# A scan layer of five engines: source order kept on every engine, preparation cut in pieces, one activation table set, pipelined epilogue

**Chip, cores, metric.** One core of a Trainium2 chip. The metric is the device time of one execution in microseconds (us), the lower the better. Executions of one kernel agree within 0.3%. The engines are named as in the profile: PE (TensorE, matrix products), DVE (VectorE), ACT (ScalarE), POOL (GpSimd) and SP (SyncE, which here issues DMA transfers). PSUM is the memory in which this kernel keeps PE's products.

## The reference, cut to what matters

Layer 0 is a two-dimensional selective scan (4 images of 48 x 48 tokens, 256 channels, 16 states, 4 scan directions). Layer 1 (attention, then spectral filters) is not touched by the change.

```python
xz = einsum('bhwc,ec->bhwe', groupnorm(x), in_proj_w); xin, z = split(xz, 2)
xc = silu(conv3x3_depthwise(xin) + conv_b)
xs = [xc in four scan orders]                       # rows, columns, and both reversed
dts_r, Bs, Cs = split(x_proj_w @ xs)
dt = softplus(dt_proj_w @ dts_r + dt_proj_b)
step: h = h * exp(dt*A) + (dt*u) * B ;  y = sum_n h * C      # along 2304 tokens
y  = sum of the four orders + D*xs
x  = x + out_proj(layernorm(y) * g + b) * silu(z))           # the epilogue
```

## The kernel before

The layer is cut into 80 *chunks* (image, direction, 480 or 384 tokens). A chunk is 8 *units* (half `h` of the channels, group `q` of 4 states). In a unit the engines work in turn: ACT makes `dA = exp(dt*A)`, DVE or POOL makes `s = dt*u*B`, DVE scans, POOL multiplies by C, PE sums over states, DVE adds to `ya`. Step sizes of the next chunk but one are prepared meanwhile, and go through DRAM to be replicated over partitions.

```python
psy = ... bufs=1 (PSUM) ; psm = ... bufs=3 (PSUM) ; s has 6 buffers

def prep(self):                      # a generator, advanced one yield per unit
    ps = x_proj @ xc;  yield
    xd = Identity(ps);  dma(bcd <- xd[32:64])                       # B and C rows to DRAM
    for h in range(NH):
        ps = dt_proj @ xd;  yield
        re[:,h,1] = Abs(ps); re[:,h,0] = Relu(ps)
    e = Exp(-e); u = e + 1;  yield
    l = Ln(u);  u = u - 1
    for h in range(NH):
        ps = e - u + l + relu   (4 matmuls);  yield                 # softplus, on PE
        re[:,h,0] = copy(ps)                                        # ACT
        re[:,h,1] = ps * x                                          # DVE
        dma(d[h] <- re[:,h]);  for c in range(4): dma(rep[h] <- d[h], replicated)   # 2 MB

def fetch(self, i):                  # broadcast row i of bcd to 128 partitions: 4 DMA issues
    t = one.tile([P, CS], tag=f"bc{i}"); ...

def enter(self):                     # unit s+2 on POOL for 3 of 8 units, else s+1 on DVE
    s = sp.tile(...)
    nc.scalar.copy(ch.entry(s), carry)                              # L344
    eng.tensor_tensor(s, rep[h][:, 1], B, mult)                     # L347
def scan(self):
    for j in range(2):
        2 x activation(dA[j], rep[h][:, 0], Exp, scale=A)           # L355
        tensor_tensor_scan(s, dA[j], s)                             # L359
def leave(self):
    nc.scalar.copy(carry, s end)                                    # L366
    nc.gpsimd.tensor_tensor(s, s, C row, mult)                      # L369
    4 x matmul(y, csum, s)                                          # L373
```

Lines are cut and shortened. All DMAs of the layer but the loads of its weights at the start are issued by SyncE (SP), one queue.

The softmax here doesn't subtract the row's maximum and nothing guards it: scores larger than these inputs give would overflow.

## Time and profile before

| | before |
|---|---|
| time, median of 3 runs | 9344.46 us |
| scan layer, start to the attention's first tokens | 5642 us |
| chunk of 480 tokens, mean of steady ones | 65.6 us |
| DVE busy in 66.03 us of such a chunk | 47.19 us |
| change of image, above three steady chunks | 111 us |

The chunk times come from the starts of the first scans of neighbouring chunks in the trace. A chunk is *steady* when it is not one of the last two of an image or the first of the next; those three together are the change of image. The lines themselves are in the prediction.

### The profile page before, as it was taken

Reading aid. Unit: us, or ns where it says so; the run is one execution under the profiler, and the core shown is the slowest. Engines: PE = TensorE matmul, PEld = TensorE weight load, DVE = VectorE, ACT = ScalarE, POOL = GpSimd, SP = SyncE. Lnnn points to the kernel's source line nnn. Section 1 sums busy time; section 2 is a strip of 40 time slices with the busy share of each in tenths; the row PEclk is TensorE's granted clock in tenths of the full one; section 3 lists DMA queues with packets and bytes.
Section 4 is the critical chain, followed back from the end, with each engine's and each line's share of the span. In section 5 each row is a group of like instructions: output and inputs, shape, how many; then the busy total and the mean of one; then the engine's idle time right before and its main releaser. Section 6 shows DMA issues by size and latency. Waiting matters only on the chain. (4 is left out here: it accounts for less than half of the span.)

```text
span 9358.5 us, 64225 instructions
## 1 busy us (share of the span) xinstructions
PE 6679.6 (71%) x22344; PEld 3265.5 (35%) x22344; DVE 4675.9 (50%) x3928; ACT 3151.3 (34%) x6187; POOL 3540.9 (38%) x984
## 2 busy tenths in 40 slices
PE   4555545555546555546555548979999999999999
PEld 1111112111112111112111114547666666666666
DVE  6777677677677776777776772021111111111111
ACT  4444445444445444445444433430000000000000
POOL 3666655666655666655666660010000000000000
PEclk6656556656556555557555559989999999999999
DMA  4434434434434434434434430000000000000000
GB/s 103 98 87 103 93 76 104 102 88 103 96 73 106 103 85 103 97 72 109 103 84 104 101 80 31 0 11 7 9 8 8 15 8 8 8 15 6 6 6 21
DMA packets 378087, 571.07 MB, mean 61 GB/s; under 512 B 50841, under 2 KB 373529, under 8 KB 377762
## 3 DMA queue, kind: packets, MB, share of 16 engines
q1 hardware_dynamic: 374784, 566.19, 26.4%
q8 instruction: 176, 2.88, 0.1%
q14 instruction: 149, 1.22, 0.0%
q10 hardware_dynamic: 2978, 0.77, 0.0%
HBM read 467.68 MB, written 99.09 MB: 61 GB/s over the span
## 5 line engine op out<-in xcount | busy, mean ns | idle before, releaser
L369 POOL TENSOR_TENSOR s<-s,bc 128x1920 f32<-128x1920 f32 (+1 forms) x640 | 2431.4, 3801 | 1904.3 <-ACT carry L366 1386.1
L359 DVE TENSOR_TENSOR_SCAN s<-dA,s 128x962 f32<-128x962 f32 (+1 forms) x1536 | 2606.7, 1744 | 434.5 <-ACT dA L355 283.7
L731 PE MATMUL cv<-tt,u 128*128 128x384 f32 (+2 forms) x9216 | 2505.5, 433 | 0.0
L373 PE MATMUL y<-s,csum 128*32 128x480 f32 (+1 forms) x5120 | 1066.9, 923 | 1344.9 <-POOL s L369 1251.2
L355 ACT ACTIVATE dA<-rep,A 128x480 f32<-128x480 f32 (+1 forms) x2560 | 1618.3, 643 | 1030.6 <-DVE s L359 999.0
L731 PEld LDWEIGHTS cv<-tt,u 128*128 128x128 f32 x9216 | 1648.7, 190 | 869.7
L737 DVE COPY U<-cv 128x384 f32<-128x384 f32 x384 | 214.0, 557 | 2245.1 <-PE cv L731 2245.1
L735 ACT COPY U<-cv 128x384 f32<-128x384 f32 x384 | 183.6, 478 | 2797.3 <-PE cv L731 2797.3
L712 POOL TENSOR_TENSOR ms<-mp,mm 128x512 f32<-128x512 f32 x16 | 20.3, 1269 | 2717.4 <-DVE G L661 2439.5
L347 POOL TENSOR_TENSOR s<-rep,bc 128x1920 f32<-128x1920 f32 (+1 forms) x240 | 981.9, 4103 | 160.8 <-DMA rep<-dtdud 114.3
L347 DVE TENSOR_TENSOR s<-rep,B 128x1920 f32<-128x1920 f32 (+1 forms) x400 | 819.5, 2064 | 437.5 <-ACT s L344 350.5
L336 PE MATMUL B<-xd,spread 32*128 32x480 f32 (+1 forms) x800 | 619.8, 871 | 429.4 <-ACT re L288 205.2
L373 PEld LDWEIGHTS y<-s,csum 128*32 128x32 f32 x5120 | 141.3, 139 | 2183.9 <-POOL s L369 1887.8
L301 PE MATMUL sp<-re,ident 128*128 128x480 f32 (+1 forms) x640 | 386.0, 712 | 194.6 <-DVE s L347 153.7
L744 PE MATMUL pr<-U,G 128*128 128x288 f32 (+1 forms) x2560 | 519.2, 358 | 0.0
L344 ACT COPY s<-carry 128x4 f32<-128x4 f32 x512 | 94.4, 193 | 1122.1 <-PE y L373 1108.7
L336 PEld LDWEIGHTS B<-xd,spread 32*128 32x128 f32 x800 | 168.8, 258 | 765.5 <-ACT re L288 304.4
L744 PEld LDWEIGHTS pr<-U,G 128*128 128x128 f32 x2560 | 407.5, 190 | 67.2
L379 DVE TENSOR_TENSOR ya<-ya,y 128x480 f32<-128x480 f32 (+1 forms) x160 | 126.7, 792 | 572.8 <-PE y L373 572.8
L285 PE MATMUL dt<-xd,dtw 9*128 9x480 f32 (+1 forms) x320 | 238.9, 841 | 222.4 <-DVE s L347 165.2
L747 DVE TENSOR_TENSOR acc<-acc,pr 128x288 f32<-128x288 f32 x512 | 232.3, 454 | 245.4 <-PE pr L744 245.4
L275 PE MATMUL xp<-xc,xw 128*64 128x480 f32 (+1 forms) x320 | 241.4, 896 | 130.8 <-DVE re L307 90.0
(154 smaller groups left out, 4689.1 us busy)
## 6 DMA issues: line engine op xcount, KB each, us to landing
rep<-dtdud SPq DMA_DIRECT2D x512, 480.0 KB, 9.1
bc<-bcd SPq DMA_DIRECT2D x1536, 60.0 KB, 2.0
dtdud<-re SPq DMA_DIRECT2D x128, 480.0 KB, 2.7
rep<-dtdud SPq DMA_DIRECT2D x128, 384.0 KB, 7.4
tt<-in_phi SPq DMA_DIRECT2D x32, 576.5 KB, 3.7
bc<-bcd SPq DMA_DIRECT2D x384, 48.0 KB, 2.0
dtdud<-re SPq DMA_DIRECT2D x32, 384.0 KB, 2.5
zd<-z SPq DMA_DIRECT2D x48, 192.0 KB, 1.9
```

The costliest lines, as they stand in the source:

```text
L275: nc.tensor.matmul(ps[:64, :n], xw[:, h, k, :], in_order(xc[h], k, self.lo, n), start=(h == 0), stop=(h == NH - 1))
L285: nc.tensor.matmul(ps[:, :n], dtw[:, k, h * P:(h + 1) * P], xd[:R + 1, :n], start=True, stop=True)
L301: nc.tensor.matmul(ps[:, :n], w, t, start=(i == 0), stop=(i == 3))
L336: nc.tensor.matmul(ps[:, :n], spread[32:64, self.q].rearrange("p c j -> p (c j)"), self.ch.xd[32:64, :n], start=True, stop=True)
L347: eng.tensor_tensor(ch.blocks(s)[:, :, ch.cols], ch.rep[self.h][:, 1, :, :n], bt[:, :n].unsqueeze(1).to_broadcast([P, G4, n]), ALU.mult)
L355: nc.scalar.activation(ch.blocks(dA[j], 2)[:, i, ch.cols], ch.rep[self.h][:, 0, g, :n], AF.Exp, scale=A[:, ch.k, self.h * G4 + g, self.q:s ...
L359: nc.vector.tensor_tensor_scan(s, dA[j][:, run], s, 0.0, ALU.mult, ALU.add)
L369: nc.gpsimd.tensor_tensor(s, s, ct[:, :n].unsqueeze(1).to_broadcast([P, G4, n]), ALU.mult)
L373: nc.tensor.matmul(ch.y[g * DL:(g + 1) * DL, :n], csum, s[:, g], start=(self.q == 0), stop=(self.q == Q4 - 1))
L731: nc.tensor.matmul(ps[:, lo - c0:CONV], u[b][:, J, g, :], taps(tt[q], lo - J * P - back, c0 + CONV - J * P - back), start=(J == 0), stop=( ...
L744: nc.tensor.matmul(ps[:, lo - lo0:hi - lo0], G[q][:, s, :], U[q][:, lo:hi], start=(q == 0), stop=(q == 1))
L747: nc.vector.tensor_tensor(o, o, ps[:, :hi0 - lo0], ALU.add)
```

## The change

Its intent: a scheduler had ordered each engine's queue by its own estimate; now the source order stands (`manual_schedule`), and the source is written so that what stands ahead in a queue is ready. The core of the diff (`...` marks cuts):

```diff
+    ctx.enter_context(tc.manual_schedule())
-    psy bufs=1, psm bufs=3
+    psy bufs=2, psm bufs=2
+    def exp_ln():
+        nc.scalar.preload_act_table_set("natural_log_exp_and_others")
...
     prep: one more yield after xd; Exp | yield | u, l, u | yield  (was: Exp, u | yield | l, u)
...
     enter(): - nc.scalar.copy(ch.entry(s), ...)
     scan():  + after the exponentials of j == 0: nc.scalar.copy(ch.entry(self.s), ...)
     leave() split: times_c (copy out, POOL product) and sum_c (PE)
...
     epilogue: stages center(i), deviation(i-1), gate(i-2), project(...) in one loop;
               gate by two scalar_tensor_tensor on DVE (was 2 on DVE, 1 on POOL); Sqrt before reciprocal
...
 def preparation(ci):
     if ci % NO == 0:
+        yield from prologue1(ci // NO)       # was one step a unit from the middle of the image
         yield from prologue2(ci // NO)
 advance: 5 steps a unit at a change of image (was 4), one piece of preparation a unit else
...
-        flush(s - 2)
-        if s: leave(s - 1)
+        if s >= 1: multiply(s - 1)
+        if s >= 2 ...: add_up(s - 2)
+        flush(s - 4)
```

More of the change, by code (lines that the diff above doesn't have):

```diff
@@ L98, in layer0 @@
     psa = ctx.enter_context(tc.tile_pool(name="psa", bufs=1, space=PSUM))
-    psy = ctx.enter_context(tc.tile_pool(name="psy", bufs=1, space=PSUM))
-    psm = ctx.enter_context(tc.tile_pool(name="psm", bufs=3, space=PSUM))
+    psy = ctx.enter_context(tc.tile_pool(name="psy", bufs=2, space=PSUM))
+    psm = ctx.enter_context(tc.tile_pool(name="psm", bufs=2, space=PSUM))
     def load(name, shape, src):
@@ L151, in layer0 @@
     nc.vector.memset(mone, -1.0)
+    eps = wp.tile([P, 1], F32, name="eps")
+    nc.vector.memset(eps, 1e-5)
     zero = wp.tile([P, G4], F32, name="zero")
@@ L216, in prologue2 @@
             nc.scalar.activation(x, x, AF.Silu)
+            exp_ln()
             xc.append(x)
             yield
-        for h in range(NH):
-            for lo in range(0, L, SUB):
+        for lo in range(0, L, SUB):
+            z = two.tile([P, NH, SUB], F32, tag="z", name=f"z{b}_{lo}")
+            for h in range(NH):
                 ps = mm_tile(f"z{b}_{lo}_{h}")
@@ L223, in prologue2 @@
                                  start=True, stop=True)
-                z = two.tile([P, SUB], F32, tag="z", name=f"z{b}_{lo}_{h}")
-                nc.scalar.activation(z, ps[:, :SUB], AF.Silu)
-                nc.sync.dma_start(zs[b][h, :, lo:lo + SUB], z)
+                nc.scalar.activation(z[:, h], ps[:, :SUB], AF.Silu)
+            nc.sync.dma_start(zs[b][:, :, lo:lo + SUB].rearrange("h p t -> p h t"), z)
+            if lo + SUB == L:
+                exp_ln()
             yield
@@ L279, in prep @@
             nc.sync.dma_start(bcd[:, :n], xd[32:64, :n])
+            yield
             u, l = [one.tile([P, NH, CS], F32, tag=f"tmp{i}", name=f"{v}{name}") for i, v in enumerate("ul")]
@@ L290, in prep @@
             nc.scalar.activation(e, e, AF.Exp, scale=-1.0)
+            yield
             nc.scalar.activation(u[:, :, :n], e, AF.Identity, bias=1.0)
-            yield
             nc.scalar.activation(l[:, :, :n], u[:, :, :n], AF.Ln)
             nc.scalar.activation(u[:, :, :n], u[:, :, :n], AF.Identity, bias=mone)
+            yield
             d = dram.tile([NH, 2, P, CS], F32, tag="dtdu", name=f"dtdud{name}")
@@ L342, in enter @@
             s = self.s = sp.tile([P, G4 * BLK + 1], F32, tag="s", name=f"s{self.name}")
-            src = zero if ch.first else carry[:, self.h, self.q]
-            nc.scalar.copy(ch.entry(s), src.unsqueeze(2))
             bt = ch.bc[self.q] if self.pool else self.bt
@@ L356, in scan @@
                                          scale=A[:, ch.k, self.h * G4 + g, self.q:self.q + 1])
+                if j == 0:
+                    src = zero if ch.first else carry[:, self.h, self.q]
+                    nc.scalar.copy(ch.entry(self.s), src.unsqueeze(2))
                 for run in ch.runs():
@@ L359, in scan, with times_c @@
                     nc.vector.tensor_tensor_scan(s, dA[j][:, run], s, 0.0, ALU.mult, ALU.add)
-        def leave(self):
+        def times_c(self):
             ch, n = self.ch, self.ch.n
@@ L366, in leave, with sum_c @@
                 nc.scalar.copy(carry[:, self.h, self.q].unsqueeze(2), s[:, :, ch.end:ch.end + 1])
-            ct = ch.bc[Q4 + self.q]
             s = s[:, :, ch.cols]
-            nc.gpsimd.tensor_tensor(s, s, ct[:, :n].unsqueeze(1).to_broadcast([P, G4, n]), ALU.mult)
+            nc.gpsimd.tensor_tensor(s, s, ch.bc[Q4 + self.q][:, :n].unsqueeze(1).to_broadcast([P, G4, n]), ALU.mult)
+        def sum_c(self):
+            ch, n = self.ch, self.ch.n
+            s = ch.blocks(self.s)[:, :, ch.cols]
             if self.q == 0:
@@ L383, in epilogue @@
         yf = [t.rearrange("p h w -> p (h w)") for t in yacc]
-        for lo in range(0, L, SUB):
-            cols = slice(lo, lo + SUB)
-            rs = one.tile([P, SUB], F32, tag="ers", name=f"rs{b}_{lo}")
-            sq = one.tile([P, NH, SUB], F32, tag="esq", name=f"sq{b}_{lo}")
-            z = [two.tile([P, SUB], F32, tag="z", name=f"zr{b}_{lo}_{h}") for h in range(NH)]
+        room = one.tile([P, L], F32, tag="xT", name=f"room{b}")
+        sqs = room[:, :2 * NH * SUB].rearrange("p (i h t) -> p i h t", i=2, h=NH)
@@ L389, in epilogue, with cols, center @@
+        rss = room[:, 2 * NH * SUB:].rearrange("p (i t) -> p i t", i=2)
+        nblk = L // SUB
+        zr = {}
+        def cols(i):
+            return slice(i * SUB, (i + 1) * SUB)
+        def center(i):
+            zr[i] = two.tile([P, NH, SUB], F32, tag="z", name=f"zr{b}_{i}")
+            nc.sync.dma_start(zr[i], zs[b][:, :, cols(i)].rearrange("h p t -> p h t"))
+            ps = psy.tile([P, 512], F32, tag="y", name=f"mu{b}_{i}")
             for h in range(NH):
-                nc.sync.dma_start(z[h], zs[b][h, :, cols])
@@ L391, in epilogue @@
-            ps = mm_tile(f"mu{b}_{lo}")
+                nc.tensor.matmul(ps[:, :SUB], dmean, yf[h][:, cols(i)], start=(h == 0), stop=(h == NH - 1))
             for h in range(NH):
-                nc.tensor.matmul(ps[:, :SUB], dmean, yf[h][:, cols], start=(h == 0), stop=(h == NH - 1))
-            for h in range(NH):
-                nc.vector.tensor_tensor(yf[h][:, cols], yf[h][:, cols], ps[:, :SUB], ALU.subtract)
-                nc.scalar.activation(sq[:, h], yf[h][:, cols], AF.Square)
-            ps = mm_tile(f"var{b}_{lo}")
@@ L398, in epilogue @@
-            for h in range(NH):
-                nc.tensor.matmul(ps[:, :SUB], dmean, sq[:, h], start=(h == 0), stop=(h == NH - 1))
-            nc.vector.tensor_scalar_add(rs, ps[:, :SUB], 1e-5)
-            nc.vector.reciprocal(rs, rs)
-            nc.scalar.activation(rs, rs, AF.Sqrt)
-            for h in range(NH):
-                v = yf[h][:, cols]
-                nc.vector.tensor_tensor(v, v, rs, ALU.mult)
-                nc.vector.tensor_scalar(v, v, ng[:, h:h + 1], nb[:, h:h + 1], ALU.mult, ALU.add)
-                nc.gpsimd.tensor_tensor(v, v, z[h], ALU.mult)
@@ L408, in epilogue, with deviation @@
-        for J in range(NJ):
-            if J % 3 == 0:
-                x = two.tile([P, 3, 2, C], F32, tag="tok", name=f"xr{b}_{J}")
-                nc.sync.dma_start(x, xs[b][:, J:J + 3])
-            ps = mm_tile(f"op{b}_{J}")
+                v = yf[h][:, cols(i)]
+                nc.vector.tensor_tensor(v, v, ps[:, :SUB], ALU.subtract)
+                nc.scalar.activation(sqs[:, i % 2, h], v, AF.Square)
+        def deviation(i):
+            ps = mm_tile(f"var{b}_{i}")
+            for h in range(NH):
+                nc.tensor.matmul(ps[:, :SUB], dmean, sqs[:, i % 2, h], start=(h == 0), stop=(h == NH - 1))
+            nc.scalar.activation(rss[:, i % 2], ps[:, :SUB], AF.Sqrt, bias=eps)
@@ L413, in epilogue, with gate, project @@
+        def gate(i):
+            rs = rss[:, i % 2]
+            nc.vector.reciprocal(rs, rs)
+            for h in range(NH):
+                v = yf[h][:, cols(i)]
+                nc.vector.scalar_tensor_tensor(v, v, ng[:, h:h + 1], rs, ALU.mult, ALU.mult)
+                nc.vector.scalar_tensor_tensor(v, v, nb[:, h:h + 1], zr[i][:, h], ALU.add, ALU.mult)
+        xr = {}
+        def project(J):
+            ps = psy.tile([P, 512], F32, tag="y", name=f"op{b}_{J}")
             for f in range(2):
@@ L416, in epilogue @@
                                      start=(h == 0), stop=(h == NH - 1))
-            t = x[:, J % 3].rearrange("p f c -> p (f c)")
+            if J % 3 == 0:
+                xr[0] = two.tile([P, 3, 2, C], F32, tag="tok", name=f"xr{b}_{J}")
+                nc.sync.dma_start(xr[0], xs[b][:, J:J + 3])
+            t = xr[0][:, J % 3].rearrange("p f c -> p (f c)")
             nc.vector.tensor_tensor(t, t, ps[:, :2 * C], ALU.add)
             if J % 3 == 2:
-                nc.sync.dma_start(mid[b][:, J - 2:J + 1], x)
+                nc.sync.dma_start(mid[b][:, J - 2:J + 1], xr[0])
+        done = 0
+        for i in range(nblk + 3):
+            if i < nblk:
+                center(i)
+            if 1 <= i <= nblk:
+                deviation(i - 1)
+            if 2 <= i <= nblk + 1:
+                gate(i - 2)
+            while done < NJ and 256 * (done + 1) <= SUB * (i - 2):
+                project(done)
+                done += 1
+        exp_ln()
     def start_y(b, xc):
@@ L451, in advance @@
             preps[ci] = preparation(ci)
-        for _ in range(4 if ci % NO == 0 else 1):
+        for _ in range(5 if ci % NO == 0 else 1):
             next(preps[ci], None)
@@ L465, in enter, with multiply @@
             units[s + 2].spread()
-    def leave(s):
+    def multiply(s):
         u = units[s]
-        y = u.leave()
-        if u.q == Q4 - 1:
-            pending.append((s, u.ch, u.h, y))
+        u.times_c()
         ci = s // len(quads) + 1
@@ L477, in leave, with add_up @@
                 chunks[ci].fetch(u.q)
+    def add_up(s):
+        u = units[s]
+        y = u.sum_c()
+        if u.q == Q4 - 1:
+            pending.append((s, u.ch, u.h, y))
     def flush(s):
@@ L484, in layer0 @@
     pending = []
-    for _ in prologue1(0):
-        pass
+    TURN = 4
     advance(0, True)
@@ L490, in layer0 @@
     yaccs[0] = start_y(0, xcs[0])
+    for j in range(TURN):
+        advance(1, False)
     for s in (-2, -1):
         enter(s)
-    opening = iter(())
     for s, unit in enumerate(units):
@@ L496, in layer0 @@
         b, i = divmod(ci, NO)
+        turned = b > 0 and i == 0 and j == 0
         enter(s)
         unit.scan()
-        flush(s - 2)
-        if s:
-            leave(s - 1)
-        if s and i == 0 and j == 0:
+        if s >= 1:
+            multiply(s - 1)
+        if s >= 2 and not (b > 0 and i == 0 and j == 1):
+            add_up(s - 2)
+        if turned:
+            add_up(s - 1)
+        flush(s - 4)
+        advance(ci + 1, j == TURN) if j <= TURN else None
+        advance(ci + 2, False) if j >= TURN else None
+        if turned:
             flush(s)
@@ L505, in layer0 @@
             yaccs[b] = start_y(b, xcs[b])
-        half = len(quads) // 2
-        if ci == 0 and j == 0:
-            advance(1, False)
-        advance(ci + 1 if j < half else ci + 2, j == half - 1)
-        if i == NO // 2 and j == 0 and b + 1 < B:
-            opening = prologue1(b + 1)
-        next(opening, None)
-    leave(len(units) - 1)
+    multiply(len(units) - 1)
+    add_up(len(units) - 2)
+    add_up(len(units) - 1)
     flush(len(units))
```

## The prediction

> **What bounds the kernel now.** I read the page first, its slices for the stages, then the busy time by window, the waits, the groups by form, and last the timeline of one chunk. The slices of the page:
>
> ```profile
> PE   4555545555546555546555548979999999999999
> DVE  6777677677677776777776772021111111111111
> ACT  4444445444445444445444433430000000000000
> POOL 3666655666655666655666660010000000000000
> PEclk6656556656556555557555559989999999999999
> ```
>
> The span has two halves. From slice 25 on (attention, then the spectral filters) PE is 9 tenths busy, and the change does not touch that code. In the first 24 slices, the scan layer, no engine is full. The scans run from 119.0 to 5577.6 us by the line view of L359, and the attention's first tokens are loaded at 5641.9 us, so 5642 us are in play and about 3700 us are not. The page's chain of what ended last names PE's convolution; it says nothing on this layer.
>
> The layer is 80 chunks (4 images, 4 directions, 5 chunks; 64 of 480 columns, 16 of 384) of 8 units each. Busy time by window, columns PE, PEld, DVE, ACT, POOL, granted clock, DMA share, GB/s; ten steady chunks and more, then one whole chunk of 480, then the last epilogue:
>
> ```profile
> 300.00:1200.00 900.00, 489.24 (x1394) 129.66 (x1394) 632.89 (x426) 433.74 (x839) 579.62 (x156) 0.59 0.44 96
> 4701.24:4767.27 66.03, 36.80 (x98) 9.03 (x98) 47.19 (x25) 31.91 (x61) 43.91 (x11) 0.58 0.44 98
> 5577.60:5641.90 64.30, 38.29 (x134) 21.25 (x134) 38.57 (x59) 9.58 (x19) 16.60 (x13) 0.74 0.44 136
> ```
>
> A chunk takes 66.03 us and its busiest engine, DVE, works 47.19 of them; POOL 43.91. So the layer is bound by waits between engines, 19 us a chunk, with DVE as the floor. The waits of 300 to 1200 us:
>
> ```profile
> PE y L373 <- POOL s L369: 210.7, 64, 11.9
> ACT s L344 <- PE y L373: 245.3, 73, 6.6
> POOL s L369 <- ACT carry L366: 243.5, 66, 12.1
> DVE ya L379 <- PE y L373: 93.0, 17, 8.5
> DVE s L347 <- ACT s L344: 76.4, 13, 7.7
> DVE s L359 <- ACT dA L355: 61.4, 32, 3.4
> ```
>
> These form a ring. The small copy that enters the carry (L344) stands in ACT's queue ahead of work that is ready; it waits for a buffer of s that PE's sum (L373) still reads, that sum waits for POOL's multiplication, and POOL waits for ACT's copy out (L366). DVE pays: of its 267 us idle in this window, 93 are the addition of y placed too early, 76 the multiplication behind the copy, 61 the exponentials. ACT's timeline in one chunk, start and length:
>
> ```profile
> 4750.03 1.28 ACT L293 ACT_TABLE_LOAD   x1
> 4751.32 1.00 ACT L293 ACTIVATE l<-u 128x960 f32<-128x960 f32 x1
> 4752.34 1.28 ACT L355 ACT_TABLE_LOAD   x1
> ...
> 4767.32 0.20 ACT L344 COPY s<-carry 128x4 f32<-128x4 f32 x1 [6.05 <-PE y L373]
> ```
>
> Two table loads sit around the logarithm, and scans waited 3.16 us just there; then the entry copy holds the queue 6.05 us.
>
> **What the Trainium skill says.** "PSUM — Partial Sum Buffer", Engine vs sequencer instructions: the queues of ScalarE, VectorE and GpSimd are strict first in, first out. The trace agrees: ready exponentials stood behind L344 for 6.05 us. So the order written into each queue is the lever, and it can also hurt. "ScalarE: Activation LUTs", What ACT_TABLE_LOAD costs and Table sets: a load is about 1283 ns, and one set holds both exp and ln. The trace has 1283 ns. "TensorE: Matmul & The Clock Gate", What's actually happening: the array is throttled when it idles and released by activity; the trace agrees, 0.58 at 56% busy here and 1.00 in the full half, so a denser layer should speed PE up a little. "SBUF — State Buffer", SBUF: two separate sides: a port pair that VectorE and GpSimd share is locked for a whole instruction. The trace fits: the 128x2304 normalisation (L195) took 4820 ns median, the same form at L210 1479. That concerns the passes of the 3x3 convolution, not the scans, which read PSUM.
>
> **The change part by part.** I compared the built order of both programs on each engine.
>
> *Order and buffers in a chunk.* L344's copy moves behind the first two exponentials and after the multiplication into s, so L347 no longer waits for it. The sum over states is issued one unit later than POOL's product, y has two PSUM tiles instead of one (the preparation two instead of three), and the addition of y comes units later. That takes away the 93 and 76 us above, and most of the ring. What stays is DVE's work by these rows (busy, mean ns of one):
>
> ```profile
> L359 DVE TENSOR_TENSOR_SCAN s<-dA,s 128x962 f32<-128x962 f32 x160 | 336.6, 2143 | 49.0 <-ACT dA L355 35.1 <-POOL s L347 13.3
> L347 DVE TENSOR_TENSOR s<-rep,B 128x1920 f32<-128x1920 f32 x50 | 106.3, 2137 | 63.7 <-ACT s L344 53.6 <-PE B L336 10.1
> L369 POOL TENSOR_TENSOR s<-s,bc 128x1920 f32<-128x1920 f32 x81 | 317.3, 3918 | 228.9 <-ACT carry L366 197.9 <-DVE s L359 20.1 <-DVE re L307 9.2
> L347 POOL TENSOR_TENSOR s<-rep,bc 128x1920 f32<-128x1920 f32 x30 | 127.2, 4255 | 0.0
> ```
>
> 16 scans x 2.10 + 5 x 2.13 + 4 small at 0.80 = 47.5 us for 480 columns. A chunk of 384, with 32 short scans, is 39.5 by the same sum.
>
> *New waits in a chunk.* Following the order by hand: with an L347 in most units, ACT's 6 us per unit hide under DVE. The tight place is the middle of a chunk. POOL must reload its broadcast row between the last product of one chunk and its first L347 of the next: 8 issues at about 0.46 us and 2.0 us to landing, some 5 us in which POOL stands. So its first product in a chunk ends about 19 us in; PE, in order, sums it (1.8), then runs the four products of each half of the step size (about 5 each), which ACT and DVE need before unit 5. I find 4 to 6 us of DVE idle there. 47.5 + 5 = 52.5 us a chunk; the short one, where all is smaller, 45.
>
> *One table set.* 224 loads become 39 in the order listing; 185 x 1.283 = 237 us of ACT time. ACT is 48% busy, so it counts only through the 3 us stall of each chunk, already inside the sum above.
>
> *Change of image.* Before, three changes of image cost about 120 us each above a steady chunk (neighbouring chunks started 96, 101 and 109 us apart instead of 62 to 66). DVE's own work there is 61 us (50 of them convolution passes) and 41 of epilogue and start. Now the next image's preparation runs 5 steps a unit in source order and the epilogue as one block with no scan between. Work 102; waits of the group norm's round trips and the first projection 30, second projection 10, gating values and step size through ACT 20; the epilogue is paced by PE (17 + 18 + 21 = 56 us of matmuls per image) rather than by DVE's 38, and about 20 of that and of its fill is extra. I take 185, that is 65 worse than before, and this is the part I know least.
>
> *Epilogue pipelined.* Only the last one is bare: 64.3 us before, 62 after. The reciprocal (2.54 us a block) stays.
>
> **Sum.** First preparation 125 + 64 x 52.5 + 16 x 45 + 3 x 185 + last epilogue 62 = 4822 us against 5642. Saved 820, so 9344 - 820 = 8524; I say 8520.
>
> **The rivals.** (1) Head-of-line blocking: in source order any late operand stops its engine though other work is ready, and the waits removed come back elsewhere, at the step size products or the B tiles with one PSUM tile fewer. For it: PE is already 56% busy at clock 0.58. Then a chunk stays near 58 to 60, 5.5 to 7.5 more than I take for 80 chunks, and the time is 8960 to 9120. (2) POOL becomes the bound: 43.9 us of work plus the 5 us reload is a floor of 49 to 50 a chunk; with it holding PE, 8400 to 8600. (3) DVE becomes the bound: chunks of 48.5, changes of image no dearer than before: 64 x 4 + 16 x 3 + 3 x 65 = 499 less, about 8020. Against it: POOL's floor. (4) The change of image is much dearer, 300 each: 8870. (5) The gain is hidden because the layer ends in something else: excluded, the attention waits for mid, and PE's later half starts when it lands.
>
> **Range and chances.** Each us per chunk is 80 us; I hold 50 to 55.5 likely, and 150 to 230 for the change of image. That gives 8320 to 8790. To lose the 2% (187 us) the layer would have to take over 5455 us, chunks of 480 near 60 us; to be slower by 2%, 5829 us and chunks near 65, about what they are. Both need the ring to come back whole elsewhere: faster 0.95, same 0.03, slower 0.02.
>
> **What would show it.** Right: chunks of 50 to 55 us; DVE 85 to 90% busy in a steady chunk; waits of ya on y and of L347 on the copy gone, what is left of DVE's idle time at the step size (L319) and at the exponentials; granted clock over 0.6; loads about 39; the half after the layer unchanged within 20 us. Wrong: chunks of 58 or more with PE or ACT as the releaser, POOL over 95%, or over 230 us at a change of image.

## The result, and the profile after

The changed kernel takes 8780.7 us (median of 4, 8776.97 to 8784.21) against 9347.33 in the same rounds: ratio 0.9394, 95% interval 0.9377 to 0.9410. A ratio here is the mean time of one kernel's fast runs over that of the other's of the same rounds, so not quite the ratio of the medians.

The 40 slices of the page after, to be laid beside those of before:

```profile
DVE  5888858888768888668888720221111111111111
POOL 3787735787736777538787600100000000000000
PEclk6666656666666666666666699999999999999999
```

DVE rises from 6 or 7 tenths to 8 in the steady slices and drops to 5, 6 or 7 at slices 6, 11 to 12 and 17 to 18: the changes of image. The next view is busy time by window, with the columns of the prediction (us, then busy us and count of PE, PEld, DVE, ACT and POOL, granted clock, DMA share, GB/s): steady chunks, then one chunk, then the last epilogue with the wait for the attention's tokens.

```profile
300.00:1000.00 700.00, 402.85 (x1292) 107.92 (x1284) 586.51 (x397) 385.62 (x763) 541.62 (x146) 0.66 0.52 115
767.41:822.36 54.95, 31.85 (x98) 8.48 (x98) 45.69 (x26) 30.26 (x61) 43.75 (x12) 0.62 0.54 118
4979.70:5058.90 79.20, 44.07 (x152) 25.61 (x144) 40.32 (x55) 11.47 (x20) 11.07 (x3) 0.67 0.38 113
```

The chunk is 54.95 us, 11.1 less, with about the same work: 43.75 us of POOL (43.91 before) and 45.69 of DVE (47.19 before). DVE's waits in it fell from 18.8 to 9.3 us. The layer now ends at 5058.9 us, 583 earlier; what follows takes 3716 us in both kernels, so all of the gain is in the layer. Which waits stay (300 to 1000 us; us in total, times, longest):

```profile
POOL s L357 <- DMA bc<-bcd: 146.4, 14, 15.4
ACT re L316 <- PE sp L313: 120.9, 26, 9.5
DVE re L319 <- ACT re L316: 71.7, 13, 6.8
ACT s L369 <- POOL s L357: 59.1, 14, 6.7
DVE s L372 <- ACT s L369: 36.9, 30, 4.2
```

The additions of y no longer wait, and DVE's multiplication hardly (4.7 us). Of DVE's 113 us idle, 72 are before the step size's product (L319) and 37 before a scan. Both go back to one thing that does not appear among the waits of 300 to 1200 us before: POOL standing for a broadcast row of B (`bc`), once a chunk, 10.5 us in the mean. The timeline of POOL shows it:

```profile
821.49 3.93 POOL L381 TENSOR_TENSOR s<-s,bc 128x1920 f32<-128x1920 f32 x1
837.06 4.23 POOL L357 TENSOR_TENSOR s<-rep,bc 128x1920 f32<-128x1920 f32 x1 [11.64 <-DMA bc<-bcd]
```

and the DMA queue of the same chunk why:

```profile
797.92 0.38 SPq L321 DMA_DIRECT2D dtdud<-re  x1
800.96 1.80 SPq L324 DMA_DIRECT2D rep<-dtdud  x4
803.40 0.38 SPq L321 DMA_DIRECT2D dtdud<-re  x1
814.08 1.78 SPq L324 DMA_DIRECT2D rep<-dtdud  x4
815.96 2.00 SPq L332 DMA_DIRECT2D bc<-bcd  x4
819.14 0.30 SPq L289 DMA_DIRECT2D bcd<-xd  x1
821.38 13.66 SPq L332 DMA_DIRECT2D bc<-bcd  x20
```

The step size is written, read back replicated, the second half's write lands 10.6 us later among those reads, its own reads follow, and 24 issues of broadcast rows come last. The first four go out right behind the reads, the next wait for reads to land: the waits of the DMA queue over the whole run have

```profile
SPq L332 <- DMA rep<-dtdud: 427.8, 228, 3.6
```

A row needs nothing from these reads. In the trace's operands each issue of SyncE signals one of eight semaphores in turn, and waits for the earlier DMA on the same one: the row issued at 826.84 takes the semaphore of the read that landed at 826.83. So at most eight of this queue's DMAs are under way at a time. From there 18 issues went out 0.46 us apart, and POOL's row, the very last, landed about 2.1 us after its last issue, at 836.7. Then POOL's two instructions (8.1 us), PE's sum and products (6.5), ACT's copy and DVE's product (1.2) lead to the next write at 852.95, one chunk (55.0 us) after that of 797.92. That has the form of a closed ring, and POOL's 43.75 us of work plus its wait of 11 is the same length.

### The profile page after: what moved, and what is told of

Its sections match the earlier page's. It is cut to its first block, busy times and chain, and to the rows that moved or that the text cites. A ratio compares the mean times of both kernels' runs of the same rounds, so it can differ in the third digit from the quotient of the medians.

```text
span 8775.2 us, 62894 instructions
## 1 busy us (share of the span) xinstructions
PE 6433.5 (73%) x22344; PEld 3227.0 (37%) x22344; DVE 4656.9 (53%) x3905; ACT 2975.0 (34%) x6001; POOL 3486.1 (40%) x936
## 4 chain that ended last, share of the span: by engine, by line
PE 48%; DMA 14%; DVE 12%; issue 6%; POOL 6%; SPq 5%; ACT 3%; POOLq 0%; DVEq 0%; ACTq 0%
PE cv L780 28%; PE pr L793 6%; DMA dtdud<-re 6%; DMA rep<-dtdud 6%; DVE s L372 5%; POOL s L381 4%; PE sp L313 4%; SPq L332 4%; PE s L605 3%; PE o L611 3%; DVE xc L221 2%; DMA bc<-bcd 2%; PE y L390 2%; DVE s L357 2%; ACT dA L365 1%
## 5 line engine op out<-in xcount | busy, mean ns | idle before, releaser
L390 PE MATMUL y<-s,csum 128*32 128x480 f32 (+1 forms) x5120 | 923.2, 817 | 1546.1 <-POOL s L381 1544.0
L365 ACT ACTIVATE dA<-rep,A 128x480 f32<-128x480 f32 (+1 forms) x2560 | 1659.2, 648 | 560.3 <-DVE s L372 515.4
L348 PE MATMUL B<-xd,spread 32*128 32x480 f32 (+1 forms) x800 | 587.1, 824 | 136.3 <-DVE s L357 123.5
L313 PE MATMUL sp<-re,ident 128*128 128x480 f32 (+1 forms) x640 | 391.0, 699 | 18.8 <-ACT re L301 12.4
L319 DVE TENSOR_TENSOR re<-sp,xc 128x480 f32<-128x480 f32 (+1 forms) x160 | 125.8, 786 | 463.8 <-ACT re L316 463.8
L348 PEld LDWEIGHTS B<-xd,spread 32*128 32x128 f32 x800 | 161.9, 251 | 501.0 <-DVE s L357 250.5
L316 ACT COPY re<-sp 128x480 f32<-128x480 f32 (+1 forms) x160 | 86.7, 542 | 733.1 <-PE sp L313 733.1
L606 ACT ACTIVATE e<-s,shift 128x512 f32<-128x512 f32 (+1 forms) x360 | 230.6, 642 | 290.7 <-PE s L605 273.8
L611 PE MATMUL o<-e,xn 128*128 128x512 f32 (+1 forms) x720 | 293.2, 550 | 0.0
```

The source lines that it names most:

```text
L313: nc.tensor.matmul(ps[:, :n], w, t, start=(i == 0), stop=(i == 3))
L348: nc.tensor.matmul(ps[:, :n], spread[32:64, self.q].rearrange("p c j -> p (c j)"), self.ch.xd[32:64, :n], start=True, stop=True)
L365: nc.scalar.activation(ch.blocks(dA[j], 2)[:, i, ch.cols], ch.rep[self.h][:, 0, g, :n], AF.Exp, scale=A[:, ch.k, self.h * G4 + g, self.q:s ...
L390: nc.tensor.matmul(ch.y[g * DL:(g + 1) * DL, :n], csum, s[:, g], start=(self.q == 0), stop=(self.q == Q4 - 1))
L611: nc.tensor.matmul(po[q][:, :w], xn[:, i // 2, i % 2, :], e[:, lo:lo + w], start=(i == 0), stop=(i == NT - 1))
```

## The experiments

Twelve kernels, each correct. Times are medians of 4 runs, ratios to the kernel before of the same rounds. Chunk means and changes of image were taken from each trace as above. The kernel before, run again in each group of rounds, had medians of 9347 to 9358 us, so differences of some 10 us between medians of different groups mean nothing. Not separated by any run: the split of PSUM between y and the preparation, the later addition of y, and the preparation's finer pieces.

| run | time, us | ratio (95%) | chunk of 480 | change of image above 3 chunks |
|---|---|---|---|---|
| changed kernel | 8780.7 | 0.9394 (0.9377 to 0.9410) | 54.60 | 201 |
| order_only | 9224.7 | 0.9858 (0.9843 to 0.9873) | 59.09 | 181 |
| no_order | 9639.7 | 1.0301 (1.0285 to 1.0316) | 69.56 | 128 |
| no_preload | 8779.6 | 0.9380 (0.9365 to 0.9396) | 54.78 | 199 |
| sum_back | 9053.8 | 0.9678 (0.9662 to 0.9694) | 58.66 | 197 |
| entry_back | 8803.4 | 0.9407 (0.9392 to 0.9423) | 54.71 | 207 |
| plain_epilogue | 8892.4 | 0.9503 (0.9489 to 0.9518) | 54.62 | 230 |
| norm_early | 8771.2 | 0.9379 (0.9365 to 0.9393) | 54.99 | 158 |
| writes_first | 8793.6 | 0.9400 (0.9386 to 0.9414) | 54.19 | 204 |
| row_first | 8628.0 | 0.9220 (0.9206 to 0.9234) | 52.79 | 201 |
| row_early | 8336.3 | 0.8907 (0.8894 to 0.8921) | 48.50 | 211 |
| both_early | 8362.6 | 0.8939 (0.8926 to 0.8952) | 48.73 | 169 |
| best | 8274.2 | 0.8842 (0.8829 to 0.8856) | 48.65 | 188 |

### The order alone, and all but the order

```diff
 order_only: the kernel before
+    ctx.enter_context(tc.manual_schedule())
 no_order: the changed kernel
-    ctx.enter_context(tc.manual_schedule())
```

> The kernel before with the one line that keeps every engine in source order, nothing else changed. If source order itself breaks the ring of waits and the moved pieces only tune it: 8900 to 9100 us, chunks of about 59. If source order alone is a head-of-line trap that needs the moved pieces (entry copy behind the exponentials, sum a unit later, second y tile): 9350 us or more.

> The changed kernel without that line, so the scheduler orders each engine again. If order is the gain: 9200 to 9400 us. If the moved pieces, the single table set and the pipelined epilogue carry the gain by themselves: 8800 to 8900 us.

Order alone gave 1.4%, between the two expectations: chunks fell to 59.09 as the first theory said, but changes of image rose from 111 to 181 us above steady chunks and ate a good part. All but the order *lost* 3.0%, which neither expectation allowed. Why is not shown; one of the longest waits there is the entry copy behind late multiplications (`ACT s L368 <- DVE s L356` at 109.5 us in 700), which the source now asks for. So the parts do not add: 1.4% and minus 3.0% apart, 6.1% together. As a whole, the moved pieces pay only in the order they were written for.

### One table set

```diff
 def exp_ln():
-    nc.scalar.preload_act_table_set("natural_log_exp_and_others")
+    pass
```

> The changed kernel without the explicit load of the table set that holds exp and ln, so some 160 to 190 loads come back, 2.57 us of ACT time in each chunk. My theory: the chunk is held by a ring through POOL's broadcast row, PE's sum, the step size and the DMA queue, and ACT has slack where the loads stand: within 30 us of the changed kernel. Rival, ACT's loads are on the path: 2.5 us x 80 chunks = 200 us slower, near 8980.

Within noise of the changed kernel, though 150 loads came back (189 against 39 in the traces). ACT's busy time in 300 to 1000 us rose from 385.62 to

```profile
300.00:1000.00 700.00, 402.23 (x1292) 108.06 (x1284) 586.62 (x397) 421.80 (x791) 541.10 (x146) 0.66 0.52 115
```

421.80 us, and DVE's stayed at 586.6. A cost taken from an engine that waits for others anyway is worth nothing here; the first theory held.

### The sum a unit later, the entry copy, the epilogue

```diff
 sum_back
-        if s >= 2 and not (...): add_up(s - 2)
-        if turned: add_up(s - 1)
+        if s >= 1: add_up(s - 1)
 entry_back
   enter(): + nc.scalar.copy(ch.entry(s), ...)   ahead of the multiplication, out of scan()
 plain_epilogue
   the old loop over blocks (subtract, square, variance, reciprocal, Sqrt, three products, the last on POOL),
   then the projection; the new z layout kept
```

> The changed kernel with PE's sum over states again right after the product of the same unit instead of a unit later. My theory, PE in source order then stands for a product that POOL has not begun and the step size products behind it come one POOL product (3.9 us) later in each chunk, on the ring: 8780 + 80 x 3.9, so 9000 to 9150. Rival, PE has room: within 50 us of the changed kernel.

> The changed kernel with the entry copy of the carry back ahead of the multiplication into s and of the exponentials, as before. My prediction counted 76 us of 900 for it, 5 us a chunk, in the kernel before. In source order the ring around it is gone (its buffer is free long before), but DVE's multiplication then waits for ACT to finish the preparation piece ahead: 0.5 to 2 us a chunk, so 8820 to 8940. Rival, the position no longer matters: within 25 us of the changed kernel.

> The changed kernel with the epilogue as it was before (block after block, gate on POOL), the rest of the change kept. In source order with no scan between, each of six blocks runs its chain alone, about 11 us against 6.5 pipelined, and the projection follows: 20 to 35 us more in each of four epilogues, so 8860 to 8920. Rival, the epilogue is paced by PE either way: under 30 us in all.

The sum's place is worth 4.06 us a chunk (58.66 less 54.60), one POOL product of 3.9, and 273 us in all: PE in order stood at a product not yet made, with the step size behind it. DVE, however, stands elsewhere than the expectation suggests: in 300 to 1000 us of `sum_back`

```profile
DVE s L357 <- POOL s L381: 98.6, 13, 13.8
```

it waits at the multiplication into s, and at the step size 10.5 us instead of 71.7. PE's B row for that unit stands behind the same sum, and in the chunk at 724 us it ended 0.1 us before the multiplication began. The entry copy's place is worth nothing clear (22.7 us in the medians, the intervals of the ratios overlap): the rival held. My reading is that the 76 us that the copy cost before belonged to the ring around it, and that the position became free once that ring was open. Source order alone did not open it: `order_only` still has `DVE s L348 <- ACT s L345` at 52.5 us in 700. Which of the other pieces did, no run shows. The pipelined epilogue is worth 112 us; the change of image grew by 29 three times, and the last epilogue from 79 to 100 us.

### What holds the chunk at 54.6 us

```diff
 row_early: two buffers for the rows that POOL multiplies into s, fetched first
-    t = one.tile([P, CS], F32, tag=f"bc{i}", ...)
+    t = (two if i < Q4 else one).tile([P, CS], F32, tag=f"bc{i}", ...)
     chunks[ci].fetch(Q4 + u.q)
-    if any(u.q == q for h, q in POOLED): chunks[ci].fetch(u.q)
+    if u.q == 0:
+        for i in sorted({q for h, q in POOLED}): chunks[ci].fetch(i)
 row_first: no second buffer, the same two statements swapped
-    chunks[ci].fetch(Q4 + u.q)
     if any(u.q == q for h, q in POOLED): chunks[ci].fetch(u.q)
+    chunks[ci].fetch(Q4 + u.q)
 writes_first: both dma(d[h] <- re[:,h]) before the first dma(rep[h] <- d[h])
```

> The changed kernel with two buffers for the two broadcast rows that POOL multiplies into s, fetched at the first unit of the second half of the chunk before instead of behind POOL's last product. My theory: POOL's 11.5 us wait for that row starts the ring (product, sum, step size, DMA write), so the chunk of 480 falls from 54.6 to 49 to 51 us and the time to 8400 to 8500. Rival, the ring is held by the writes and replicated reads in the DMA queue whatever POOL does: chunks stay over 53 and the time over 8650.

> The changed kernel with two statements swapped: POOL's broadcast row is fetched just before, not just behind, the row of C that waits for POOL's own last product; no second buffer. If POOL's 11.5 us wait is mostly standing in the queue behind that gated row and its four issues, the wait falls to 3 to 6 us and the chunk from 54.6 to 49.5 to 52, time 8420 to 8600. If the row has to wait for the replicated reads to land anyway, the chunk stays over 53.5 and the time over 8700.

> The changed kernel with both step size writes of a chunk issued before either replicated read, so the second write no longer lands behind 2 MB of reads (10.5 us to landing). If the DMA queue is part of the ring: 1 to 3 us less a chunk, 8550 to 8700. If POOL's row, which waits for POOL's own last product and eight issues, sets the ring alone: within 30 us of the changed kernel.

`row_early` takes 444 us off the changed kernel, more than expected, and a chunk falls to 48.50 us. Its steady stretch, the same 700 us:

```profile
300.00:1000.00 700.00, 471.13 (x1470) 126.63 (x1462) 654.13 (x435) 430.40 (x849) 614.43 (x164) 0.69 0.60 131
```

DVE is busy 654 of 700 us, 93%, and its two waits left are a fraction of before:

```profile
POOL s L357 <- DMA bc<-bcd: 47.5, 10, 9.4
DVE re L319 <- ACT re L316: 31.6, 13, 5.3
```

So the row POOL waits for set the chunk; that theory held, and the steady chunk is now near DVE's own work (45.8 us of 48.5).

`row_first` missed what it was expected to bring, and is the more telling for it. The gain is 1.81 us a chunk, which is four issues of 0.46 us (1.84), the four it was moved ahead of. My reading, that the row stands mostly behind the product gating its neighbour, was wrong: in the traces the issues run with hardly a gate (8.3 us of waits for POOL in 700) from the landing of the replicated reads on, and the row pays for its place in that queue. The issues from the landing of the last read to the row's last one, in one chunk of the changed kernel, `row_first` and `row_early`:

```profile
826.84 8.20 SPq L332 DMA_DIRECT2D bc<-bcd  x18
809.60 6.33 SPq L332 DMA_DIRECT2D bc<-bcd  x14
807.31 2.16 SPq L332 DMA_DIRECT2D bc<-bcd  x5
```

`row_early` moves the row ahead of twelve issues of other rows and of the write of `bcd` too: 13 fewer, 6.0 us, and the gain is 6.1. Over the chunks in which POOL waits there (77, 77 and 65 of 80) the median time from the last read's landing to POOL's multiplication is 10.25, 8.33 and 4.11 us, 1.9 and 6.1 less: the chunk of 480 became shorter by as much (1.8 and 6.1).

`writes_first` came within the expectation of the rival, and yet does not speak for it. The second write now lands in 3.0 us instead of 10.6 in the chunk of the timeline, as wanted; the medians of both writes and of the reads over all chunks of 480 (9.7 and 8.2 in the changed kernel):

```profile
dtdud<-re SPq DMA_DIRECT2D x128, 480.0 KB, 3.0
rep<-dtdud SPq DMA_DIRECT2D x512, 480.0 KB, 11.6
```

but the reads land in 11.6 us instead of 8.2: all eight are now issued together, and they land one after another, 2.4 us apart. In the trace the last of the eight landed at 826.25, against 826.83 in the changed kernel with the first write issued at 797.98 and 797.92. What the experiment took away was a wait, not the 4 MB behind it. POOL now waits for the reads themselves (173.6 us in the run, 10.4 in the changed kernel). Chunks of 480 became 0.4 us shorter, those of 384 2.2 us longer (49.59 against 47.41). The experiment cannot tell whether the reads belong to the ring; the timeline and the stretch measured above, which begins where they land, say that they do. No run made the reads smaller or gave the rows a queue of their own.

### The change of image

```diff
 norm_early: transposes and group norm of the next image one step a unit from mid image, as before
-        yield from prologue1(ci // NO)
+    if i == NO // 2 and j == 0 and b + 1 < B: opening = prologue1(b + 1)
+    next(opening, None)
-    5 steps a unit
+    4 steps a unit
 both_early: row_early and norm_early
```

> The changed kernel with the next image's transposes and group norm taken out of its change of image and done one step a unit from the middle of the image, as the kernel before does. A change of image costs 201 us above steady chunks, of which DVE sits 26.5 us behind the transposes' loads and some 10 more in the norm. My theory, steps packed five to a unit expose their round trips: 35 to 45 us less at each of three changes, so 8640 to 8680. Rival, the change of image is bound by the work of the 3x3 convolution and the epilogue: under 10 us each, over 8750.

> Rows early (48.5 us a chunk, 8336 us) and norm early together. If the two costs are apart, the gains add: norm_early's gain on top of 8336, near 8215. If the change of image is then bound by DVE's own work, less: 8280 to 8336.

The change of image did get 43.5 us shorter, as the first theory said, and the total did not move. The starts of chunks tell why: the chunk in the middle of the second image, which now has the transposes beside it, takes 87.6 us instead of 50.0, and the one after it 61.8 instead of 54.9. The scans in the middle of the first image wait once for 18.24 us: PE in order stands for the load of x, ACT behind PE, the exponentials behind ACT (`PE tr L182 <- DMA x<-in_x` at most 18.2 us at once). The round trip is paid in this place as in the other. With the chunk shorter (`both_early`) the total is 26 us worse than without it, outside both expectations.

### A version that beats both

```diff
 best: row_early, and
+    load_x(b + 1) at mid image: the three loads of x, ahead of the transposes at the change of image
+    load_xr(0), load_xr(3) at the start of the epilogue
+    gating values silu(z): two blocks a unit in units 4 to 6 of the image's last chunk, out of prologue2
```

> Rows early (8336), and the change of image eased where its trace shows waits for loads and packed pieces: x of the next image loaded half an image ahead, the residual x of the epilogue loaded at its start, the gating values two blocks a unit in the last units of the image. Loads account for about 30 us of a change of image and 14 of an epilogue, the packed gating values for about 15: 8336 - 3 x 45 - 14, so 8160 to 8240, which beats both kernels by over 5%. Rival, the waits move to the next operand in the in-order queues as in norm_early: over 8300.

8274.2 us: 11.6% below the kernel before, 5.8% below the changed one. It lies between the two expectations: the change of image lost 23 us, not 45, the last epilogue 10 (77.3 to 67.3), and 14 were given back before the first scan (155.4 against 141.2), where the gating values of the first image now stand by themselves. The three pieces were not tried one by one.

## Why the prediction was right, and where its sum was off

The result is inside the range, by 9 us, and 261 us above the point. All the terms of the sum erred to the same side, and that the range held by 9 us is luck in part; the mechanism held better than the sizes. By its own steps:

- **Bound by waits between engines, DVE as the floor: right.** With POOL's rows fetched first into two buffers, the chunk goes to 48.50 us beside the 47.5 that the prediction counted as DVE's work (it added single durations, which overlap a little: the trace has 45.8 us busy).
- **Waits removed (y, L347, the ring): right,** and their size roughly: the chunk lost 11 us. The sizes put to single pieces did not hold: the entry copy's place alone is worth nothing clear, the table set nothing (as said), the order alone 1.4%.
- **New waits in a chunk, 5 us: the mechanism right, the term mis-sized.** The prediction named POOL's broadcast row as what opens the new waits and set it at "some 5 us in which POOL stands", 8 issues and a landing. POOL stood 11.64 us in the chunk shown and 11.14 in the one before. The count was of the 8 issues between the last product and the row; 18 issues stand between the landing of 4 MB of replicated reads and POOL's multiplication. Rival (2), POOL's work plus the reload as a floor, is what happened: 43.75 + 11 instead of 43.9 + 5. This gives 54.6 instead of 52.5 for 480 tokens and 47.4 instead of 45 for 384: 134 + 38 us of the 237 by which the layer ended late. (All terms give 255; the first and the last chunk, 46.1 and 44.3 us, give 19 back.)
- **Change of image, 185 us: 201,** 48 us in three. The largest wait of DVE there, 26.5 us behind the load of x for the transposes, it had not named. It took the change before at about 120 us, where the traces give 111.
- **First preparation 125, last epilogue 62: 141.9 and 79.2.** The epilogue was taken as slightly faster than before (64.3), and is slower: in source order none of it starts until the last sum is in (DVE waits 12.05 us for it), and it stands twice about 5 us for its residual load. In source order the plain epilogue is slower still (100). `no_order`, the same pipelined code under the scheduler, has 58.8 against 64.3 before, so what made the last epilogue slower is the order, not the pipelining.
- **Signs to look for:** 39 loads, clock 0.66, an untouched second half (3716 us in both): right. DVE at 85 to 90%: 84. What is left was to be at L319: 72 of 113 us are; the rest is not at the exponentials but at the entry copy behind POOL's late product.

What stays open: whether the last part of POOL's wait in `row_early` (47.5 us in 700) still costs anything, since DVE is 93% busy there; and how much of a change of image must remain, of which DVE's own work is about 109 us by the trace (246.5 us busy in the three chunks, less three of 45.7); the prediction had 102.

## What to carry to other kernels

When a scheduler's order is replaced by the source's, write down for each queue, the DMA queue too, what stands ahead of each late operand: the new bound here was a 240 KB row at the end of 24 issues, invisible in the busy times, and moving its fetch was worth 444 us beside the 567 of the whole change. In this kernel, in source order, the round trip for x cost the same in either of two places. And a wait that vanishes (a landing of 10.6 us become 3.0) proves nothing when the same bytes still have to pass.

## What the Trainium skill lacked or had wrong

- "ScalarE: Activation LUTs", What ACT_TABLE_LOAD costs, gives 1283 ns and a drain of about 1380 ns, 2.66 us a switch. The loads here took 1283 ns, but with no drain to be seen: in `no_preload` the load at 829.46 us followed an instruction of 1.00 us that began at 828.44, and the next began at 830.76. The switch cost 1.3 us on ACT, and nothing in the time of this kernel.
- "DMA: Bandwidth & Descriptors" gives a fixed cost near 2.0 us (Anatomy of one DMA), for DMAs issued from GpSimd; here a row's 60 KB quarter, issued from SyncE once the replicated reads had landed, took 1.8 to 2.2 us to land, about the same. I found no figure there for the spacing of consecutive issues from SyncE: 0.46 us for these rows, and 18 of them stood in the ring. Rows issued while replicated reads were in flight landed after up to 11 us.
- Not lacking, but leaned on: "TensorE: Matmul & The Clock Gate", What's actually happening (activity releases the throttle), agrees in direction; the mean granted clock rose with the layer's density, 0.59, 0.66 and 0.69 (before, changed, rows early).
- Likewise "SBUF — State Buffer", SBUF: two separate sides (whichever of VectorE and GpSimd takes the shared port pair first has it for its whole instruction), agrees with the convolution passes on DVE, 2579 ns at least and 6462 at most in the changed kernel, 3.9 us apart, which is one POOL product. No run isolated it.
